# Gathering the first 42 chunks of edge rows from the raw input, and scaling them in their buffers

## The chip, the core and the metric

One core of one Trainium2 chip runs the whole program. The metric is the device time of one execution in microseconds (us); the median of three timed executions is quoted, and one further execution was taken with the hardware profiler. The engines have the profile's names: PE (matrix), PEld (its weight loads), DVE (vector), ACT (scalar), POOL (GpSimd) and SP (which here only issues DMAs).

## What is computed

`x` has 6250 rows (nodes) of 256 floats. `src` and `dst` list 106250 directed edges, sorted by `dst`. With `ln` a row normalization without gain:

```python
y    = ln(x)
h    = segment_sum((y @ W)[src] * rsqrt(max(out_deg, 1))[src], dst) * rsqrt(max(in_deg, 1)) + b
x2   = x + relu(h)
out  = x2 + moe(ln(x2))      # 8 experts, top 2 of them for each row, 256 -> 1024 -> 256 with gelu
```

`out_deg` counts how often a node stands in `src`, `in_deg` how often in `dst`. The matrix product with `W` is linear, so the kernel sums scaled rows of `y` first and multiplies by `W` after the sum.

## The kernel before

**Prologue (the source count).** All 831 chunks of 128 source numbers (the last holds 10) are loaded as `flat`. DVE splits each number into a low part (7 bits) and a high part (0 to 48), and for 32 chunks at a time (26 rounds, `counts`) writes two one-hots: `oh_hi` (L305, 128 x 1568, bf16) and `oh_lo` (L310, 128 x 4096, bf16), each in two buffers. PE multiplies the two, chunk by chunk, into `hist` (L316), a 128 x 49 table of out-degrees that lies in one PSUM tile. Beside this ACT takes the sums of the 49 tiles of `x` (`xres`, L368), then the sums of squares (L378); PE turns the edge lists by transposes (`turn`, L332, eight turns) so that `srcT` (row numbers, one column for each chunk) and `relT` (position of the target in a 128-wide window) come out with edges on partitions; POOL turns the integer lists into floats (`s_f` L274, `dst_f` L275) and makes small constants (`after`, `ones`, `tok1`, ...). In the fourth turn (`n == 3`) a product with `ones` gives `total` (L394), the number of edges that lie within their windows. The order on each engine is the order of the program text (`manual_schedule`).

When `hist` is complete, DVE works out a scale and a shift for each node (`scale0`, `shift0`, L418 and L420). DVE, ACT and POOL scale the 49 tiles of `xres` in place (L429, L434, L424), and SP writes them in seven groups to the DRAM table `ytab` (L436). Then all engines read `flag_i` and pass a branch (L443) that handles edges outside of their windows; with this input it isn't taken.

**Edge phase.** 831 chunks of 128 edges follow, 14 to a block, 60 blocks. For chunk i POOL gathers 128 rows of `ytab` by an indirect DMA into `msg[i % NMSG]` (`gather`, L1064); column 256 of every `msg` tile is 1. DVE makes one-hots of the window positions for seven chunks at a time (`oh`, L1075). PE adds `oh`.T @ `msg` into `pm` (L1135, 128 x 257: sums and in-degree). After each block `finish` (L600 to L612) transposes `pm` into a ring of node columns; when a tile of 128 nodes is complete, `tile_sums` (L646, L650) multiplies by `W`; when a group of tiles is complete, `route_group` chooses experts, and its rows are sent to the DRAM table `xs` by indirect DMAs on POOL (L825). The experts' products (`ph` L996, `py` L1013) are woven between the chunks at a planned rate, and their results are added to `out` by indirect DMAs on POOL (L1035).

POOL's order is written out by the main loop: `gather(0..11)` ahead of it, and then, at chunk i, `gather(i + LEAD)` with `LEAD = 12`, followed by at most one of the waiting `xs` sends or `out` adds. `NMSG` is 28. A gather waits until the matmul that read its buffer before is done.

**Tail.** When the edges are used up, the remaining expert steps run back to back.

Of the kernel before, what the change touches and what calls it, by code (L numbers as in the profile page):

```python
# [23 lines left out]
def gnn_then_moe(  # L24
# [47 lines left out]
    MW = D + 4  # L72
    NMSG = 28
    LEAD = 12
# [76 lines left out]
    split = LASTROWS // 32 * 32  # L151

    edges = ctx.enter_context(tc.tile_pool(name="edges", bufs=1))
    srcT = edges.tile([P, NCOL], I32, name="srcT")
# [31 lines left out]
    xres = early.tile([P, NT, D], F32, name="xres")  # L186
    dst_f = early.tile([NBE, BE], F32, name="dst_f")
    inside = early.tile([NBE, BE], F32, name="inside")
    flag_i = early.tile([1, 1], I32, name="flag_i")
    starts = list(range(0, NCP, GC))  # L190

    with tc.manual_schedule(), tc.tile_pool(
# [14 lines left out]
        iota_hi = hl.tile([P, NHI, GC], BF16, name="iota_hi")  # L207
        in_rows = {n: rows.tile([NBE, BE], I32, name=f"{n}_rows") for n in ("src", "dst")}
        zeros = const.tile([P, SB * XW], F32, name="zeros")
# [6 lines left out]
        nc.vector.memset(zeros, 0.0)  # L216

        nc.sync.dma_start(flat[:, :FULL], src[: FULL * P].rearrange("(p c) -> p c", p=P))
# [4 lines left out]
        for name, v in (("src", src), ("dst", dst)):  # L223
            nc.scalar.dma_start(
                in_rows[name][: NBE - 1, :],
                v[: (NBE - 1) * BE].rearrange("(p c) -> p c", c=BE),
            )
            nc.scalar.dma_start(
                in_rows[name][NBE - 1 : NBE, :LASTE],
                v[(NBE - 1) * BE :].rearrange("(p c) -> p c", p=1),  # L230
            )
# [40 lines left out]
        steps_of(pcol, [[0, 1]], 0, 1)  # L272
        s_f = rows.tile([NBE, BE], F32, name="s_f")
        nc.gpsimd.tensor_copy(s_f, in_rows["src"])  # L274
        nc.gpsimd.tensor_copy(dst_f, in_rows["dst"])  # L275
        steps_of(iota_w, [[1, WIN]])
        after = const.tile([P, P], F32, name="after")
        nc.gpsimd.memset(after, 1.0)
# [15 lines left out]

        for op, by, to in ((ALU.bitwise_and, LO - 1, lo), (ALU.logical_shift_right, 7, hi)):
            part = rows.tile([P, NCP], I32, tag="part", name="part")
            nc.vector.tensor_scalar(part, flat, by, None, op0=op)
            nc.vector.tensor_copy(to, part)
        hist = s1h.tile([P, NT], F32, name="hist")
# [36 lines left out]

        counts(14)

# [36 lines left out]
        for n, one in enumerate(turns):  # L375
            turn(*one)
            for _, t in zip(range(share), squares):
                nc.scalar.activation(junk, xres[:, t, :], AF.Square,  # L378
                                     bias=mean_n[:, t : t + 1], accum_out=sqs[:, t : t + 1])
            counts(1)  # L380
            if n == 3:

                wrow = rowsp.tile([1, P], F32, tag="wrow", bufs=1, name="wrow")
                nc.tensor.transpose(wrow[:, :NBE], win_f, ident[:NBE, :NBE])
                within = rows.tile([NBE, 1], F32, name="within")
                nc.vector.tensor_scalar(
                    inside, rel, 0.0, float(WIN - 1), op0=ALU.max, op1=ALU.min
                )
# [27 lines left out]
        nc.vector.tensor_scalar(deg, hist, 1.0, None, op0=ALU.max)  # L416
        scale0 = rsqrt(rows, deg, NT, "ns")
        nc.vector.tensor_tensor(scale0, scale0, rs0, ALU.mult)  # L418
        shift0 = rows.tile([P, NT], F32, name="shift0")
        nc.vector.tensor_tensor(shift0, mean_n, scale0, ALU.mult)  # L420
        for g in range(NG):
            for t in range(g * GT, (g + 1) * GT):
# [15 lines left out]
                xres[:, g * GT : (g + 1) * GT, :],  # L438
            )


# [96 lines left out]
    ringp = ctx.enter_context(tc.tile_pool(name="ring", bufs=2))  # L538
    msgp = ctx.enter_context(tc.tile_pool(name="msg", bufs=1))
    selp = ctx.enter_context(tc.tile_pool(name="sel", bufs=3))  # L540
# [26 lines left out]
    nc.vector.memset(gone_to[0], 0.0)  # L567
    msg = [msgp.tile([P, MW], F32, name=f"msg{i}") for i in range(NMSG)]
    for i in range(NMSG):
        nc.vector.memset(msg[i][:, D : D + 1], 1.0)  # L570
    scatters, bases, adds, reads = [], [], [], []
# [671 lines left out]
```

## Time and profile before

| | us |
|---|---|
| median of three executions | 1839.8 (1833.39 to 1840.7) |
| the profiled execution, device time | 1838.93 |
| its span in the profile | 1837.1 |
| last scale and shift ready, scaling of `xres` begins | 114.25 |
| first gather is issued on POOL | 138.13 |
| first `pm` matmul | 145.32 |
| first send to `xs` | 311.39 |
| last `pm` matmuls | 1535 |

How to read it: the span is what the profiler covers from the first instruction to the last, and it lies 1.8 us under the device time of the same execution. A row of the timeline begins with its start and its duration in us, and a bracket at its end tells how long the engine had been idle and what ended that. A row of the windows' table has each engine's busy time in the stretch with the number of instructions, then the granted PE clock as a share of full speed (PEclk), the DMA engines' busy share and the rate in GB/s. The list of waits has total us, number of waits and the longest. Busy PE time is modelled: a matmul at the lower clock shows as a longer one.

### The profile page before, as it was taken

How to read it: one execution, taken by the hardware profiler on the slowest of the kernel's cores; microseconds unless marked ns; L12 is line 12 of the kernel's file. 1: busy time of each engine (PE TensorE's matmuls, PEld its weight loads, DVE VectorE, ACT ScalarE, POOL GpSimd, SP SyncE). 2: the span in 40 equal slices, each digit the busy share in tenths (PEclk: the TensorE clock that was granted, in tenths of full speed). 3: DMA queues.
4: the chain of work that ended last, by engine and by line, in shares of the span. 5: the costliest groups of instructions: out<-in, count | busy, mean ns of one | idle time of the engine just before them, and what ended most of it. 6: DMA issues, size and time to landing. Idle time of an engine off the chain costs nothing.

```text
span 1837.1 us, 21552 instructions
## 1 busy us (share of the span) xinstructions
PE 1525.5 (83%) x7076; PEld 1245.8 (68%) x7076; DVE 822.4 (45%) x2971; ACT 340.8 (19%) x869; POOL 1112.2 (61%) x1063
## 2 busy tenths in 40 slices
PE   6846786666798688797987989999798977999996
PEld 6833344344587577676876878878687865788885
DVE  9961226145136237264363363735545476321111
ACT  2740001001112102121120121212112121222221
POOL 1007776776774776776767767777777773222222
PEclk9998777676798799898998999999999987999998
DMA  4645433343663664655756748576576642756662
GB/s 144 250 142 180 114 112 111 101 151 96 220 207 118 187 215 150 203 175 183 223 152 213 219 152 280 168 221 215 164 215 201 218 153 60 239 181 201 209 193 68
DMA packets 119173, 321.68 MB, mean 175 GB/s; under 512 B 20918, under 2 KB 74100, under 8 KB 112140
## 3 DMA queue, kind: packets, MB, share of 16 engines
q1 hardware_dynamic: 58784, 183.17, 27.9%
q0 software_dynamic: 60144, 136.19, 27.4%
q8 instruction: 59, 0.97, 0.2%
q10 hardware_dynamic: 124, 0.85, 0.1%
q14 instruction: 62, 0.51, 0.1%
HBM read 268.07 MB, written 52.05 MB: 174 GB/s over the span
## 4 chain that ended last, share of the span: by engine, by line
PE 57%; DMA 15%; DVE 11%; issue 5%; POOL 3%; ACT 1%; POOLq 0%; DVEq 0%; ACTq 0%
PE ph L996 18%; PE py L1013 17%; PE pm L1135 14%; DMA msg<-ytab,srcT 11%; POOL msg L1064 3%; DMA xs<-rowt,pos_i 2%; DMA out_x<-yo,to_i 2%; PE misc L646 2%; PE misc L714 1%; PE misc L723 1%; PE ptf L952 1%; PE misc L606 1%; DVE xeT L972 1%; PE misc L607 1%; PE misc L650 1%
## 5 line engine op out<-in xcount | busy, mean ns | idle before, releaser
L1064 POOL DMA_INDIRECT msg<-ytab,srcT x831 | 818.6, 985 | 272.6 <-issue 128.0
L1135 PE MATMUL pm<-msg,oh 128*128 128x257 f32 x1662 | 570.1, 439 | 148.1 <-DMA msg<-ytab,srcT 135.4
L1135 PEld LDWEIGHTS pm<-msg,oh 128*128 128x128 f32 x1662 | 330.4, 214 | 267.9 <-DMA msg<-ytab,srcT 168.1
L996 PE MATMUL ph<-xeT,w 128*128 128x256 f32 x1728 | 442.7, 395 | 59.1 <-DVE xeT L972 59.0
L1013 PE MATMUL py<-w,hT 128*128 128x256 f32 x1728 | 436.0, 388 | 0.0
L996 PEld LDWEIGHTS ph<-xeT,w 128*128 128x128 f32 x1728 | 339.4, 199 | 112.2 <-DVE xeT L972 64.7
L1013 PEld LDWEIGHTS py<-w,hT 128*128 128x128 f32 x1728 | 327.8, 195 | 41.6 <-DVE yb L1024 0.6
L1003 ACT ACTIVATE hT<-ph,w 128x256 f32<-128x256 f32 x432 | 180.7, 470 | 797.5 <-PE ph L996 627.6
L1035 POOL DMA_INDIRECT out_x<-yo,to_i x108 | 174.9, 1619 | 253.1 <-DVE yo L1029 227.5
L612 DVE TENSOR_TENSOR ring<-ring,misc 128x384 f32 x60 | 33.3, 555 | 411.9 <-PE misc L607 411.5
L825 POOL DMA_INDIRECT xs<-rowt,pos_i x98 | 101.7, 1038 | 87.7 <-issue 46.1
L1075 DVE TENSOR_TENSOR oh<-iota_w,relT 128x896 f32<-128x896 f32 (+1 forms) x119 | 126.6, 1077 | 33.4 <-PE pm L1135 32.8
L960 DVE SCALAR_TENSOR_TENSOR to_i<-xin,to 128x2 int32<-128x2 f32 x54 | 8.9, 164 | 258.1 <-DMA out_x<-yo,to_i 257.0
L316 PE MATMUL hist<-oh_hi,oh_lo 128*128 128x49 bf16 x831 | 85.0, 279 | 21.4 <-DVE oh_lo L310 21.2
L316 PEld LDWEIGHTS <-oh_lo 128*128 128x128 bf16 x831 | 81.5, 150 | 24.0 <-DVE oh_lo L310 23.2
L600 ACT COPY ag<-pm 128x257 f32<-128x257 f32 x60 | 22.5, 374 | 345.0 <-PE pm L1135 306.3
L1024 DVE TENSOR_TENSOR yb<-py,w 128x512 f32<-128x512 f32 x54 | 37.1, 688 | 68.0 <-PE py L1013 67.9
L646 PE MATMUL misc<-gw_sb,ring 128*128 128x256 f32 x196 | 56.4, 413 | 6.6 <-DVE ring L612 6.6
L310 DVE TENSOR_TENSOR oh_lo<-iota_lo,src_lo 128x4096 bf16<-128x4096 bf16 x26 | 59.4, 2286 | 0.0
L972 DVE TENSOR_SCALAR xeT<-ptf,w 128x256 f32<-128x256 f32 x108 | 53.7, 539 | 9.3 <-PE ptf L952 9.3
L725 ACT COPY xtT<-misc 128x256 f32<-128x256 f32 x49 | 18.2, 372 | 180.1 <-PE misc L723 180.1
L646 PEld LDWEIGHTS misc<-gw_sb,ring 128*128 128x128 f32 x196 | 38.7, 205 | 18.6 <-DVE ring L612 13.6
(531 smaller groups left out, 1054.5 us busy)
## 6 DMA issues: line engine op xcount, KB each, us to landing
w<-in_wcat SPq DMA_DIRECT2D x54, 2182.0 KB, 9.3
xin<-xs SPq DMA_DIRECT2D x54, 260.0 KB, 3.7
msg<-ytab,srcT POOLq DMA_INDIRECT x831, 2.9
strayT<-zeros SPq DMA_DIRECT2D x1, 9216.0 KB
ytab<-xres SPq DMA_DIRECT2D x7, 896.0 KB, 6.8
ring<-strayT SPq DMA_DIRECT2D x4, 1536.0 KB
x<-in_x SPq DMA_DIRECT2D x48, 128.0 KB, 10.2
out_x<-x SPq DMA_DIRECT2D x48, 128.0 KB, 2.1
```

Of the source, the lines that this page charges most:

```text
L310: nc.vector.tensor_tensor(oh_lo, iota_lo, lo[:, None, c0 : c0 + GC].to_broadcast([P, LO, GC]), ALU.is_equal,)
L316: nc.tensor.matmul(hist, oh_lo[:, :, c], oh_hi[:, :, c], start=(c0 + c == 0), stop=(c0 + c == NCH - 1),)
L646: nc.tensor.matmul(pw[:, :D], sums[:, k, c0 : c0 + P], gw_sb[:, k, :], start=(k == 0), stop=(k == KD - 1),)
L825: sc = nc.gpsimd.indirect_dma_start(out=xs, out_offset=bass.IndirectOffsetOnAxis(ap=pos_i[:, j : j + 1], axis=0), in_=rowt[:, i, :], in_of ...
L972: nc.vector.tensor_scalar(xeT[:, k, :], pt[:, k, :], w[:, OG + k : OG + k + 1], w[:, OB + k : OB + k + 1], op0=ALU.mult, op1=ALU.add,)
L996: nc.tensor.matmul(ph[:, c - c0, :], w[:, k * H + c * P : k * H + (c + 1) * P], xeT[:, k, :], start=(k == 0), stop=(k == KD - 1),)
L1003: nc.scalar.activation(hT[:, c, :], ph[:, c - c0, :], AF.Gelu, bias=w[:, OB1 + c : OB1 + c + 1],)
L1013: nc.tensor.matmul(py[:, s, :], hT[:, c, s * P : (s + 1) * P], w[:, OW2 + c * D : OW2 + (c + 1) * D], start=(c == 0), stop=(c == HC - 1),)
L1035: ad = nc.gpsimd.indirect_dma_start(out=out, out_offset=bass.IndirectOffsetOnAxis(ap=to_i[:, s : s + 1], axis=0), in_=yo[:, s, :], in_offs ...
L1064: nc.gpsimd.indirect_dma_start(out=msg[i % NMSG][:, :D], out_offset=None, in_=ytab, in_offset=bass.IndirectOffsetOnAxis(ap=srcT[:, c : c + ...
L1075: nc.vector.tensor_tensor(oh[:, :n, :], iota_w[:, None, :].to_broadcast([P, n, WIN]), relT[:, c : c + n, None].to_broadcast([P, n, WIN]), ...
L1135: nc.tensor.matmul(pm, oh_of[b, half][:, j % HALF, :], msg[i % NMSG][:, : D + 1], start=(j == 0), stop=(i + 1 == end_of[b]),)
```

## The change

The first 42 chunks are gathered from `x` itself, not from `ytab`, and POOL issues these gathers early in the prologue, as soon as their row numbers are there. The rows arrive unscaled, so each needs scale and shift of its source node. These are picked for each edge with one-hots: 42 transposed low-part one-hots (`loT`) select by a matmul the 2 x 49 candidates, and a product with the high-part one-hot (`ohe_hi`) and a sum leave one value. The float32 table is split into three bf16 parts that are added in PSUM.

- The row numbers come by their own small load, `first_i` (42 x 128), first on ACT's queue; ACT turns them into floats, PE transposes them, ACT writes them back as integers (`firstT`).
- `NMSG` becomes 42. The `msg` tiles are allocated at the start; POOL sets their column of ones behind the 42 gathers, where DVE did it after the branch.
- The casts of the edge lists go from POOL to ACT, in place. Their loads are split in 48 and 11 rows.
- Between the fifth and the sixth round of the count DVE makes the one-hots of the 42 chunks, PE transposes them, ACT copies them out of PSUM.
- The product with `ones` (`total`) moves from the fourth turn to the sixth.
- Behind the scaling of `xres`, nine groups of up to five chunks are picked and scaled, a third of the chunks on DVE, the others on ACT.
- In the main loop the first 42 gathers are gone; `gather(i + LEAD)` begins with `gather(42)` at i = 30.

```diff
-    NMSG = 28
+    NMSG = 42
...
+        first_i = rows.tile([NMSG, P], I32, name="first_i")
+        nc.scalar.dma_start(first_i, src[: NMSG * P].rearrange("(c p) -> c p", p=P))
...
-            nc.scalar.dma_start(
-                in_rows[name][: NBE - 1, :],
-                v[: (NBE - 1) * BE].rearrange("(p c) -> p c", c=BE),
-            )
+            for b0, b1 in ((0, 48), (48, NBE - 1)):
+                nc.scalar.dma_start(
+                    in_rows[name][b0:b1, :],
+                    v[b0 * BE : b1 * BE].rearrange("(p c) -> p c", c=BE),
+                )
...
-        nc.gpsimd.tensor_copy(s_f, in_rows["src"])
-        nc.gpsimd.tensor_copy(dst_f, in_rows["dst"])
         steps_of(iota_w, [[1, WIN]])
+        first_f = rows.tile([NMSG, P], F32, name="first_f")
+        nc.scalar.copy(first_f, first_i)
+        ptF = rowsp.tile([P, 4, P], F32, tag="ptE", name="ptF")
+        nc.tensor.transpose(ptF[:, 0, :NMSG], first_f, ident[:NMSG, :NMSG])
+        firstT = rows.tile([P, NMSG], I32, name="firstT")
+        nc.scalar.copy(firstT, ptF[:, 0, :NMSG])
+        nc.scalar.copy(s_f, in_rows["src"])
+        nc.scalar.copy(dst_f, in_rows["dst"])
+        for i in range(NMSG):
+            nc.gpsimd.indirect_dma_start(
+                out=msg[i][:, :D], out_offset=None, in_=x,
+                in_offset=bass.IndirectOffsetOnAxis(ap=firstT[:, i : i + 1], axis=0),
+            )
+        for i in range(NMSG):
+            nc.gpsimd.memset(msg[i][:, D : D + 1], 1.0)
...
-        counts(14)
+        counts(5)
+        ident_b = rows.tile([P, P], BF16, name="ident_b")
+        nc.vector.tensor_copy(ident_b, ident)
...
+        digits(firstT, lo_e, hi_e, NMSG)
...
+        for c0 in range(0, NMSG, GC):
+            n = min(GC, NMSG - c0)
+            oh_lo = s1o.tile([P, LO, GC], BF16, tag="oh_lo", name="oh_lo")
+            nc.vector.tensor_tensor(
+                oh_lo[:, :, :n], iota_lo[:, :, :n],
+                lo_e[:, None, c0 : c0 + n].to_broadcast([P, LO, n]), ALU.is_equal,
+            )
+            nc.vector.tensor_tensor(
+                ohe_hi[:, :, c0 : c0 + n], iota_hi[:, :, :n],
+                hi_e[:, None, c0 : c0 + n].to_broadcast([P, NHI, n]), ALU.is_equal,
+            )
+            for d0 in range(0, n, 4):
+                m = min(4, n - d0)
+                ptb = rowsp.tile([P, 4, P], BF16, tag="ptB", name="ptB")
+                for d in range(d0, d0 + m):
+                    nc.tensor.transpose(ptb[:, d - d0, :], oh_lo[:, :, d], ident_b)
+                nc.scalar.copy(loT[:, c0 + d0 : c0 + d0 + m, :], ptb[:, :m, :])
+        counts(9)
...
-            if n == 3:
+            if n == 5:
...
+        for q in range(3):
+            nc.vector.tensor_copy(parts[q], rest if q else both)
+            if q < 2:
+                nc.vector.tensor_tensor(rest, rest if q else both, parts[q], ALU.subtract)
...
+        PK = 5
+        per_edge = rows.tile([P, NMSG, 2], F32, name="per_edge")
+        for c0 in range(0, NMSG, PK):
...
+            for c in range(n):
+                for q in range(3):
+                    nc.tensor.matmul(
+                        pk[:, c], loT[:, c0 + c, :], parts[q], start=(q == 0), stop=(q == 2)
+                    )
+            prod = rows.tile([P, PK, 2, NT], F32, tag="prod", name="prod", bufs=2)
+            nc.vector.tensor_tensor(
+                prod[:, :n], pk,
+                ohe_hi[:, :, c0 : c0 + n].rearrange("p t c -> p c t")[:, :, None, :]
+                .to_broadcast([P, n, 2, NT]), ALU.mult,
+            )
+            nc.vector.tensor_reduce(per_edge[:, c0 : c0 + n, :], prod[:, :n], AX.X, ALU.add)
+            for c in range(c0, c0 + n):
+                if c % 3 == 0:
+                    nc.vector.tensor_scalar(
+                        msg[c][:, :D], msg[c][:, :D], per_edge[:, c, 0:1],
+                        per_edge[:, c, 1:2], op0=ALU.mult, op1=ALU.add,
+                    )
+                else:
+                    nc.scalar.activation(msg[c][:, :D], msg[c][:, :D], AF.Identity,
+                                         bias=per_edge[:, c, 1:2], scale=per_edge[:, c, 0:1])
...
-    for i in range(LEAD):
-        gather(i)
...
         if i + LEAD < NCK:
-            gather(i + LEAD)
+            if i + LEAD >= NMSG:
+                gather(i + LEAD)
```

More of the change, by code (lines that the diff above doesn't have):

```diff
@@ L151, in gnn_then_moe @@
     split = LASTROWS // 32 * 32
+    msgp = ctx.enter_context(tc.tile_pool(name="msg", bufs=1))
+    msg = [msgp.tile([P, MW], F32, name=f"msg{i}") for i in range(NMSG)]
+    assert NMSG <= NCH - 1 and NMSG <= 2 * GC
     edges = ctx.enter_context(tc.tile_pool(name="edges", bufs=1))
@@ L186, in gnn_then_moe @@
     xres = early.tile([P, NT, D], F32, name="xres")
-    dst_f = early.tile([NBE, BE], F32, name="dst_f")
-    inside = early.tile([NBE, BE], F32, name="inside")
+    in_rows = {n: early.tile([NBE, BE], I32, name=f"{n}_rows") for n in ("src", "dst")}
+    s_f, dst_f = (in_rows[n][:].bitcast(F32) for n in ("src", "dst"))
+    inside = s_f
     flag_i = early.tile([1, 1], I32, name="flag_i")
@@ L207, in gnn_then_moe @@
         iota_hi = hl.tile([P, NHI, GC], BF16, name="iota_hi")
-        in_rows = {n: rows.tile([NBE, BE], I32, name=f"{n}_rows") for n in ("src", "dst")}
         zeros = const.tile([P, SB * XW], F32, name="zeros")
@@ L272, in gnn_then_moe @@
         steps_of(pcol, [[0, 1]], 0, 1)
-        s_f = rows.tile([NBE, BE], F32, name="s_f")
-        nc.gpsimd.tensor_copy(s_f, in_rows["src"])
-        nc.gpsimd.tensor_copy(dst_f, in_rows["dst"])
         steps_of(iota_w, [[1, WIN]])
+        first_f = rows.tile([NMSG, P], F32, name="first_f")
[13 more added lines that the diff above has]
+            nc.gpsimd.memset(msg[i][:, D : D + 1], 1.0)
         after = const.tile([P, P], F32, name="after")
@@ L292, in gnn_then_moe, with digits @@
         steps_of(step_no, [[1, MMAX]])
[L295 to L298, printed above, removed]
+        def digits(v, lo, hi, n):
+            for op, by, to in ((ALU.bitwise_and, LO - 1, lo), (ALU.logical_shift_right, 7, hi)):
+                part = rows.tile([P, NCP], I32, tag="part", name="part")[:, :n]
+                nc.vector.tensor_scalar(part, v, by, None, op0=op)
+                nc.vector.tensor_copy(to, part)
+        digits(flat, lo, hi, NCP)
         hist = s1h.tile([P, NT], F32, name="hist")
@@ L335, in turn @@
             nc.scalar.copy(to[:, j0 : j0 + m, :], pt[:, :m, :NBE])
-        counts(14)
+        counts(5)
+        ident_b = rows.tile([P, P], BF16, name="ident_b")
+        nc.vector.tensor_copy(ident_b, ident)
+        lo_e = rows.tile([P, NMSG], BF16, name="lo_e")
+        hi_e = rows.tile([P, NMSG], BF16, name="hi_e")
+        digits(firstT, lo_e, hi_e, NMSG)
+        loT = rows.tile([P, NMSG, P], BF16, name="loT")
+        ohe_hi = rows.tile([P, NHI, NMSG], BF16, name="ohe_hi")
+        for c0 in range(0, NMSG, GC):
[16 more added lines that the diff above has]
+        counts(9)
         late = rows.tile([NBE, 1], F32, name="late")
@@ L416, in gnn_then_moe @@
         nc.vector.tensor_scalar(deg, hist, 1.0, None, op0=ALU.max)
-        scale0 = rsqrt(rows, deg, NT, "ns")
-        nc.vector.tensor_tensor(scale0, scale0, rs0, ALU.mult)
-        shift0 = rows.tile([P, NT], F32, name="shift0")
+        both = rows.tile([P, 2, NT], F32, name="both")
+        scale0, shift0 = both[:, 0, :], both[:, 1, :]
+        nc.vector.tensor_tensor(scale0, rsqrt(rows, deg, NT, "ns"), rs0, ALU.mult)
         nc.vector.tensor_tensor(shift0, mean_n, scale0, ALU.mult)
+        rest = rows.tile([P, 2, NT], F32, name="rest")
+        parts = [rows.tile([P, 2, NT], BF16, name=f"part{q}") for q in range(3)]
+        for q in range(3):
+            nc.vector.tensor_copy(parts[q], rest if q else both)
+            if q < 2:
+                nc.vector.tensor_tensor(rest, rest if q else both, parts[q], ALU.subtract)
         for g in range(NG):
@@ L439, in gnn_then_moe @@
             )
+        PK = 5
+        per_edge = rows.tile([P, NMSG, 2], F32, name="per_edge")
+        for c0 in range(0, NMSG, PK):
+            n = min(PK, NMSG - c0)
+            pk = rowsp.tile([P, 4, P], F32, tag="ptE", name="pk").rearrange("p a b -> p (a b)")[
+                :, : n * 2 * NT
+            ].rearrange("p (c h t) -> p c h t", c=n, h=2)
+            for c in range(n):
[19 more added lines that the diff above has]
+                                         bias=per_edge[:, c, 1:2], scale=per_edge[:, c, 0:1])
     n_stray = nc.values_load(flag_i[0:1, 0:1], min_val=0, max_val=NCOL * P)
@@ L538, in gnn_then_moe @@
     ringp = ctx.enter_context(tc.tile_pool(name="ring", bufs=2))
-    msgp = ctx.enter_context(tc.tile_pool(name="msg", bufs=1))
     selp = ctx.enter_context(tc.tile_pool(name="sel", bufs=3))
@@ L567, in gnn_then_moe @@
     nc.vector.memset(gone_to[0], 0.0)
-    msg = [msgp.tile([P, MW], F32, name=f"msg{i}") for i in range(NMSG)]
-    for i in range(NMSG):
-        nc.vector.memset(msg[i][:, D : D + 1], 1.0)
     scatters, bases, adds, reads = [], [], [], []
```

## Prediction

> **What bounds the kernel now.** I began with the windows, cut at the stages: prologue, table and branch, edges before and after the first routing, edges with experts, tail.
>
> ```profile
> 0.00:115.00 115.00, 89.39 (x862) 85.47 (x862) 105.92 (x121) 58.95 (x207) 13.26 (x20) 1.00 0.46 158
> 115.00:145.00 30.00, 0.00 (x0) 0.00 (x0) 13.84 (x57) 6.24 (x13) 9.29 (x12) 1.00 0.85 287
> 145.00:311.00 166.00, 127.38 (x354) 73.73 (x354) 55.40 (x194) 8.16 (x22) 123.29 (x125) 0.75 0.41 123
> 480.00:1540.00 1060.00, 931.11 (x4292) 786.09 (x4292) 513.81 (x2083) 194.94 (x455) 777.86 (x740) 0.93 0.61 190
> 1540.00:1837.00 297.00, 271.96 (x1270) 237.95 (x1270) 75.97 (x309) 63.87 (x152) 62.97 (x42) 0.95 0.55 171
> ```
>
> The prologue is DVE's (106 of 115 us), with POOL idle for 100 us of it. From 145 to 311 nothing looks full. POOL's timeline shows why:
>
> ```profile
> 138.13 1.18 POOL L1064 DMA_INDIRECT msg<-ytab,srcT  x1 [19.49 <-SPq L443]
> 145.32 2.05 PE L1135 MATMUL pm<-msg,oh 128*128 128x257 f32 x4 [34.51 <-DMA msg<-ytab,srcT]
> 192.98 0.95 POOL L1064 DMA_INDIRECT msg<-ytab,srcT  x1 [0.31 <-issue]
> 194.24 0.95 POOL L1064 DMA_INDIRECT msg<-ytab,srcT  x1 [0.30 <-issue]
> 311.39 1.01 POOL L825 DMA_INDIRECT xs<-rowt,pos_i  x1 [5.30 <-issue]
> ```
>
> A gather takes 0.95 us and the next begins 0.30 us later: POOL is full at 1.26 us a chunk though its busy share reads 0.76. PE waits for it:
>
> ```profile
> PE pm L1135 <- DMA msg<-ytab,srcT: 61.7, 45, 34.5
> ```
>
> (waits of PE from 145 to 312; 34.5 us of them is the wait for the first chunk.) PE could go faster: six chunks that lay ready at 151.94 took 3.83 us, 0.64 each at full clock; at 210.71, in a stretch with gaps, three took 3.16, 1.05 each. So POOL sets the pace until the first routing. There it stops: at 311.39 it waits 5.3 us for positions that PE, DVE and ACT work out behind chunk 97.
>
> **What it removes.** From POOL's edge queue, 42 gathers. The 42 gathers before 194.24 are the ones taken out (the windows count 42 from 137 to 194), so gather 42 begins at 194.24 now. In the changed program it is the first on POOL behind the branch, and waits only for its buffer: for the first `pm` matmul, which ends 0.9 us after it begins. If that matmul came at 145.3 as now, gather 42 would come at 146.2, 48.0 us sooner. From there POOL's order is what it was, LEAD still 12, so whatever gather 42 gains is kept as long as POOL paces: **gain = 48.0 - d**, d being what the prologue adds ahead of the first `pm`.
>
> Does PE keep up? It must be through chunk 97 when gather 97 lands, 55 x 1.26 + 4 = 73 us after the first `pm`. A block is 14 x 0.64 + 1.3 (two transposed groups, 0.63 and 0.64) + about 1.3 for tiles (L646 1.13, L650 0.38 each) = 11.5 us, 0.82 a chunk, 80 us for 98, if all of these rows, taken from half-clock stretches, stay; at 0.75 it is even with POOL. So PE may cost up to 7 us; at 1.05 a chunk throughout it would cost 30. I take 0.
>
> Later stages keep the shift: order of chunks, sends, adds and experts is unchanged, and the ring of 28 or 42 never binds with a lead of 12. The tail's work is the same.
>
> **What it adds to the prologue (d).**
>
> ```profile
> 16.80 2.28 DVE L310 TENSOR_TENSOR oh_lo<-iota_lo,src_lo 128x4096 bf16<-128x4096 bf16 x1
> 28.56 1.82 POOL L274 CAST s_f<-src_rows 60x1792 f32<-60x1792 int32 x1 [20.57 <-DMA src_rows<-in_src]
> 29.15 2.07 DVE L305 TENSOR_TENSOR oh_hi<-iota_hi,src_hi 128x1568 bf16<-128x1568 bf16 x1 [0.34 <-PE hist L316]
> 114.25 10.67 DVE L429 TENSOR_SCALAR xres<-xres,ns_r,shift 128x256 f32<-128x256 f32 x28
> ```
>
> 1. *PE's head.* The transpose of `first_f` now stands first on PE, and all of `hist` behind it. ACT makes `first_f` only after issuing its loads, the last of which wait for the first two `x` loads: the trace has these landing at 8.97 and, but for one part, 11.55. With ACT's table load (1.28 us) and two small copies PE starts at 15.0 instead of 12.55: +2.4. Bound: ACT was held in its last issue until 23.8; were it again, +14.
> 2. *The edge one-hots.* DVE: one `oh_lo` and `oh_hi` in full (3.3) and one of 10/32 (1.0), casts 0.9. PE's transposes go through two PSUM buffers that ACT empties eleven times; the relT copy of 240 numbers takes 0.60, so 0.7 each for 512; the sixth count round waits for the first eight. Walked through with two buffers, that round ends at 38.9 instead of 31.3 (28.0 for the fifth, and one round of 3.3): +7.6. Two rounds get 1.1 us back each, as POOL's casts no longer hold DVE (the row at 29.15 took 2.07 where others take 0.97): +5.4 in all (4 to 8). Here ACT must have its casts done, and for that `dst` must have landed. Before, 59 rows landed at 28.5 (`src`) and 49.2 (`dst`), 413 KB in 20.6 us; 896 KB of `x` on 128 rows landed within 7.3. I take the 48 rows to be nearer to the latter; if not, ACT, the copies, PE and `hist` stand until 53: about +21.
> 3. *POOL is late for `total`.* `ones` is set behind the 42 gathers and 42 memsets (42 x 0.06 by DVE's row for them, 2.5), PE waits for it in the sixth turn, with `hist` rounds behind. When does POOL get there? Gathers beside DVE:
>
> ```profile
> 187.27 2.06 DVE L1075 TENSOR_TENSOR oh<-iota_w,relT 128x896 f32<-128x896 f32 x2
> 188.37 1.79 POOL L1064 DMA_INDIRECT msg<-ytab,srcT  x1 [0.30 <-PE pm L1135]
> 190.47 0.95 POOL L1064 DMA_INDIRECT msg<-ytab,srcT  x1 [0.30 <-DMA msg<-ytab,srcT]
> ```
>
> A gather that begins under a DVE product of two SBUF tensors stands until that ends and then takes 0.83; it gets in even between two that stand back to back (139.62: 1.22). In the count DVE does nothing else, `oh_hi` 0.9 then `oh_lo` 2.2 us. A gather let in when `oh_lo` ends is done 0.83 later, and the next asks after 1.13: too late for the end of `oh_hi`, unless DVE paused 0.33 for PE, as in every second round. So three gathers in two rounds (6.6 us): 23 by the end of the fourteenth round (65), 5 more by the turns (77), two a turn (4 us each): 40 by 101, done at 104, `ones` at 109, where PE wanted it at 104: +5. With one a round it is +17; with 1.26 us throughout, done at 68, 0.
>
> The Trainium skill speaks against this placing: "SBUF — State Buffer", "Who interferes with whom", says that a GpSimd instruction reading SBUF fully blocks beside such a DVE operation, and the page's summary advises against hiding a POOL-issued DMA under DVE's fast modes. By its example (3.1 us for a DMA beside a DVE copy, 0.62 alone), an estimate of 3.4 us a gather leaves 16 for after 103 and makes this term 20, the sum 1818. The trace's gathers wait only for the instruction under way; that decides.
>
> 4. *Three bf16 parts*: five operations of about 0.24: +1.2.
> 5. *Picking and scaling*, behind the scaling of `xres`: 8.4 groups on DVE, each a product of 490 (nearest row: 512 in 0.69), a sum of 490 (nearest: 40 in 0.18; by length 0.7), 1.67 scalings at 0.38 to 0.41: 2.07 us, 17.4 in all; then `oh` 1.05 and a start, 18.9 from the last scaling to the first `pm`. Now it is 145.32 - 124.92 = 20.4 (table landing, branch, gather): -1.5. The table's writes hide most of it: they held the branch until 137.4. Without reductions at that speed +5; at least 12.5 (branch) + 1.8, so -6. ACT's 28 scalings at 0.50 (14) run beside. PE's 126 small products fit between.
>
> Sum: d = 2.4 + 5.4 + 5 + 1.2 - 1.5 = 12.5. Gain 48.0 - 12.5 = 35.5; the profiled execution was 1838.9 (span 1837.1 and 1.8 around it), 0.9 under the median. So 1803.
>
> **Rivals.**
> - *A smaller gain*: one gather a round (+12), or PE at 0.95 a chunk (93 us against 73 to chunk 97, -20): gain 24 to 16, 1815 to 1823. For it: PE's clock share of 0.75 here. Against: the gaps that go with it are POOL's.
> - *The loads don't split*: terms 1 and 2 become 14 and 21 with overlap, d about 34, 1825.
> - *Slower*: gathers get in only when DVE pauses. About 12 would be through at the sixth turn, and PE stands for 30 x 1.26 + 5 = 43 us: d = 50; with the chain of term 5 at +5 it is 57, so 1848. It decides from d = 48. For it: the gather stretched to 1.79. Against: the back-to-back rows.
> - *No effect on the end*: the head start is given back at 311, where POOL waits for routing. Against: that wait ends a chain from chunk 97, which itself waited for its gather (266.8, landing 269.5).
>
> **How the numbers follow.** Forecast (gain 25 to 47) 0.63; smaller gain or unsplit loads 0.20; slower 0.09; given back within 9 us 0.08, a part of which may fall on either side. About 0.5% (9 us) is what a measurement of this kernel can tell from no change. All low bounds together (0 from term 1, 4, 0, 1.2, -6) give d = -1, 1790; the high end takes in one gather a round with a PE cost, and unsplit loads: 1826.
>
> **What would show it.** In the profile after: `hist` beginning near 15; `dst` landed before 20; 42 gathers from 15 on, three in two rounds, ended near 104; `total` waiting for POOL about 5 us; scaling of `xres` at 126; first `pm` near 157, gather 42 within 1 us of it and then 1.26 us apart; first send near 275; last `pm` near 1500; a tail as long as now. It is wrong if gathers in the count take over 3.3 us each, if PE and not POOL paces chunks 42 to 97, or if the distance from the first send to the end is not 1526 us.

## The result and the profile after

| | before | after |
|---|---|---|
| median, us (13 runs each, side by side) | 1840.70 | 1821.32 |
| lowest to highest, us | 1833.39 to 1850.43 | 1811.36 to 1830.20 |
| the profiled execution, us | 1838.93 | 1816.55 |
| its span, us | 1837.1 | 1814.8 |
| mean granted PE clock | 0.903 | 0.918 |

The ratio is 0.9894, with a 95% interval of 0.9872 to 0.9915: the changed kernel is about 1.1% (19 us; 22 in the profiled pair) faster. The prediction was 1803, a gain of 36; its range, 1790 to 1826, holds the result. So the direction was right and the size was not.

The windows of the changed kernel, cut at the same stages (the prologue to the scaling, the picks, the edges to the first send, the edges with experts, the tail; columns as before):

```profile
0.00:138.00 138.00, 96.36 (x906) 90.73 (x907) 109.06 (x129) 68.21 (x222) 94.42 (x102) 1.00 0.54 171
138.00:172.00 34.00, 11.79 (x127) 10.50 (x126) 32.73 (x65) 21.22 (x42) 3.79 (x7) 1.00 0.60 194
172.00:290.00 118.00, 96.60 (x355) 67.35 (x356) 57.98 (x197) 8.16 (x22) 86.44 (x88) 0.84 0.46 143
459.00:1518.00 1059.00, 927.32 (x4282) 782.29 (x4280) 514.03 (x2077) 194.80 (x455) 776.39 (x740) 0.94 0.61 191
1518.00:1815.00 297.00, 272.01 (x1270) 237.70 (x1270) 75.92 (x309) 63.88 (x152) 62.92 (x42) 0.95 0.55 171
```

The stage from the first chunk to the first send took 166 us and takes 118. The last two windows, set 21 and 22 us earlier than those of the kernel before, have the same busy times as there (POOL 776 and 778, PE 927 and 931; in the tail PE 272 and 272). The prologue and the picks take 172 where the prologue and the wait for the table took 145. POOL, idle for 100 us of the old prologue, is now busy for 94 us of it. In the timelines of PE and POOL of the changed kernel (start, duration, instruction) these are the first `pm` matmuls, gathers 42 and 90, and the first send:

```profile
171.86 9.50 PE L1216 MATMUL pm<-msg,oh 128*128 128x257 f32 x32 [6.11 <-DVE oh L1157]
173.33 1.18 POOL L1146 DMA_INDIRECT msg<-ytab,srcT  x1 [31.55 <-PE pm L1216]
235.97 0.95 POOL L1146 DMA_INDIRECT msg<-ytab,srcT  x1 [0.30 <-issue]
289.64 1.04 POOL L907 DMA_INDIRECT xs<-rowt,pos_i  x1 [4.02 <-issue]
```

The first `pm` is at 171.86 (before 145.32). Gather 42, now POOL's first, follows at 173.33, where it stood at 194.24: 20.9 us earlier. PE runs through 16 chunks that lie ready in the first row, and the 42 chunks take it 23.3 us, 0.556 each. By chunk 90 it has caught up with POOL: gather 90 begins at 235.97, its matmul at 238.8. The first send is 21.8 us earlier (311.39 to 289.64), the last `pm` 22.1 (1535.0 to 1512.9), the end 22.3. PE's waits between the first chunk and the first send:

```profile
PE pm L1216 <- DMA msg<-ytab,srcT: 9.2, 17, 1.1
```

This wait for gathered rows was 61.7 us with the first chunk. It is 9.2, and POOL still sets the pace behind it.

Where the missing 14 us are is seen in the prologue. PE's waits up to the first `pm`:

```profile
PE ptF L286 <- ACT first_f L284: 19.6, 1, 19.6
PE total L444 <- POOL ones L305: 11.1, 1, 11.1
```

PE's first instruction waits until 19.6 for ACT, and `total` waits 11.1 us for `ones`. ACT's timeline shows the first of the two (ACTq is the issue of a DMA):

```profile
17.63 0.23 ACTq L236 DMA_DIRECT2D dst_rows<-in_dst  x1
17.89 1.28 ACT L284 ACT_TABLE_LOAD   x1 [17.89 <-DMA xres<-in_x]
19.19 0.30 ACT L284 CAST first_f<-first_i 42x128 f32<-42x128 int32 x1
22.92 1.73 ACT L290 CAST dst_rows<-dst_rows 60x1792 f32<-60x1792 int32 x1 [1.14 <-DMA dst_rows<-in_dst]
```

The last load of `dst` rows waited for the second group of `x` until 17.63, and `first_f` stands behind it. `dst` had landed by 22.92, where it landed at 49.2 in the kernel before: the split loads came in time.

### The profile page after: what moved, and what is told of

Its sections match the earlier page's. It is cut to its first block, busy times and chain, and to the rows that moved or that the text cites. A ratio compares the mean times of both kernels' runs of the same rounds, so it can differ in the third digit from the quotient of the medians.

```text
span 1814.8 us, 22012 instructions
## 1 busy us (share of the span) xinstructions
PE 1512.6 (83%) x7245; PEld 1252.7 (69%) x7245; DVE 847.4 (47%) x2989; ACT 365.0 (20%) x912; POOL 1149.8 (63%) x1103
## 4 chain that ended last, share of the span: by engine, by line
PE 58%; DMA 13%; DVE 11%; issue 5%; POOL 2%; ACT 1%; DVEq 0%; POOLq 0%; ACTq 0%
PE ph L1078 19%; PE py L1095 17%; PE pm L1216 15%; DMA msg<-ytab,srcT 10%; PE misc L728 2%; DMA out_x<-yo,to_i 1%; DMA xs<-rowt,pos_i 1%; POOL msg L1146 1%; PE misc L796 1%; PE misc L805 1%; PE ptf L1034 1%; PE misc L688 1%; PE misc L689 1%; DVE xeT L1054 1%; POOL xs L907 1%
## 5 line engine op out<-in xcount | busy, mean ns | idle before, releaser
L1146 POOL DMA_INDIRECT msg<-ytab,srcT x789 | 777.5, 985 | 272.3 <-issue 121.6
L1216 PE MATMUL pm<-msg,oh 128*128 128x257 f32 x1662 | 542.4, 426 | 102.9 <-DMA msg<-ytab,srcT 85.2
L1095 PE MATMUL py<-w,hT 128*128 128x256 f32 x1728 | 431.3, 385 | 0.0
L1095 PEld LDWEIGHTS py<-w,hT 128*128 128x128 f32 x1728 | 323.7, 192 | 41.6 <-DVE yb L1106 0.5
L1157 DVE TENSOR_TENSOR oh<-iota_w,relT 128x896 f32<-128x896 f32 (+1 forms) x119 | 126.7, 1077 | 21.5 <-PE pm L1216 21.1
L292 POOL DMA_INDIRECT msg<-in_x,firstT x42 | 84.4, 2010 | 24.8 <-issue 12.5
L1054 DVE TENSOR_SCALAR xeT<-ptf,w 128x256 f32<-128x256 f32 x108 | 53.7, 539 | 8.9 <-PE ptf L1034 8.9
```

Source lines behind the costliest of these rows:

```text
L292: nc.gpsimd.indirect_dma_start(out=msg[i][:, :D], out_offset=None, in_=x, in_offset=bass.IndirectOffsetOnAxis(ap=firstT[:, i : i + 1], axi ...
L1054: nc.vector.tensor_scalar(xeT[:, k, :], pt[:, k, :], w[:, OG + k : OG + k + 1], w[:, OB + k : OB + k + 1], op0=ALU.mult, op1=ALU.add,)
L1095: nc.tensor.matmul(py[:, s, :], hT[:, c, s * P : (s + 1) * P], w[:, OW2 + c * D : OW2 + (c + 1) * D], start=(c == 0), stop=(c == HC - 1),)
L1146: nc.gpsimd.indirect_dma_start(out=msg[i % NMSG][:, :D], out_offset=None, in_=ytab, in_offset=bass.IndirectOffsetOnAxis(ap=srcT[:, c : c + ...
L1157: nc.vector.tensor_tensor(oh[:, :n, :], iota_w[:, None, :].to_broadcast([P, n, WIN]), relT[:, c : c + n, None].to_broadcast([P, n, WIN]), ...
L1216: nc.tensor.matmul(pm, oh_of[b, half][:, j % HALF, :], msg[i % NMSG][:, : D + 1], start=(j == 0), stop=(i + 1 == end_of[b]),)
```

## Experiments

All are edits of the changed kernel. The theory is that of the prediction, gain = 48.0 - d, with d made too small in its terms 1, 3 and 5. The rival is that the shorter prologue doesn't reach the end, or that the terms overlap and don't add up.

The first four runs (`e1_head` to `e4_no_stt`) were made on a chip on which the kernel before took 2246 us, with PE's clock granted at 0.84; their times can't be set beside the others, but their prologues can, since DVE's, ACT's and POOL's rows there have the same durations (`oh_lo` 2.28, a gather alone 0.95).

### ACT's copies ahead of the waiting loads (e1_head)

`row_loads` and `last_row` hold the row loads as they were; the last two of `dst` (11 rows and 522 numbers) now stand behind the two copies:

```diff
+        row_loads("src", src, slice(0, 2))
+        last_row("src", src)
+        row_loads("dst", dst, slice(0, 1))
...
         nc.scalar.copy(firstT, ptF[:, 0, :NMSG])
+        row_loads("dst", dst, slice(1, 2))
+        last_row("dst", dst)
         nc.scalar.copy(s_f, in_rows["src"])
```

> Made from the changed kernel: ACT copies first_f and firstT before it issues the last two loads of dst rows (11 rows and 522 ids), so the transpose at the head of PE's queue no longer waits for loads of x. Theory (step 1 of the sum is mis-sized because ACT's two issues stand behind x groups 0 and 1): first_f is done by about 7, hist starts near 12.6 as in the kernel before, instead of 19.86, and the gathers start near 9 instead of 20.45. The prologue gains the 7.3 us of hist, and 4 to 6 us more because the gathers end some 12 us earlier and total waits for ones 5 to 7 us instead of 11.1: first pm at 158 to 161 instead of 171.9, median near 1809. Rival A (PE's first step is not what the prologue hangs on, the DVE's one-hots are): first pm stays above 168, median near 1820. Rival B (the prologue gets shorter but the end does not follow it): first pm falls as in the theory, the median stays near 1821.

Measured: 2233.5 us, ratio to the kernel before on that chip 0.9987 (0.9935 to 1.0039). PE's timeline at the start:

```profile
7.52 0.33 PE L292 MATMUL ptF<-ident,first_f 42*128 42x42 f32 x1 [7.52 <-POOL ident masks.py:199]
12.54 3.68 PE L348 MATMUL hist<-oh_hi,oh_lo 128*128 128x49 bf16 x35 [4.69 <-DVE oh_lo L342]
```

`hist` begins at 12.54, as in the kernel before, and the first `pm` comes at 161.9 instead of 171.9. Of these 9.9 us, 7.3 are the head, and nearly all of the rest is a shorter wait of `total` (8.6 instead of 11.1; 5 to 7 were expected, so the first `pm` lies just outside 158 to 161). Term 1 is confirmed; rival A falls. On that chip the end didn't follow, which is what rival B said. PE's waits from 160 to 330, and the rows of ACT and PE at the longest of them ("issue" and "remote" stand where the profile shows nothing that ended the wait):

```profile
PE misc L696 <- issue: 46.6, 3, 21.1
```

```profile
198.66 0.38 ACT L690 COPY ag<-pm 128x257 f32<-128x257 f32 x1 [27.46 <-remote]
199.09 0.69 PE L696 MATMUL misc<-ident,ag 128*128 128x128 f32 x2 [21.05 <-issue]
```

PE stood three times, up to 21.1 us. Each time it went on 0.06 us after ACT's copy of a finished block's sums (`ag`), which PE transposes. In the rows shown the copy began 20.6 us after PE's matmuls had ended (178.03), with ACT idle; what held it the profile doesn't show. Between the stops PE wasn't always slower: 28 `pm` matmuls in a row took 6.23 us here as in the profile after. From 200 to 250 its clock was granted at 0.74, where the profile after has 0.81, and chunk 120 was multiplied 48.6 us after its gather began (274.1 to 322.7), in the profile after 10.7 (273.8 to 284.5). From the first `pm` to the first send 165.9 us passed, 48 more than the 117.8 of the profile after, and the three stops make up 46.6. So the edges hung on PE there and not on POOL, as in the prediction's rival of a slow PE, but by these stops, which that rival didn't have; that the lower clock causes them isn't shown. The changed kernel itself wasn't run on that chip. Nor do the four runs made there order by their first `pm`: it is at 161.9, 162.3, 174.0 and 177.6 for ratios of 0.9987, 0.990, 0.9934 and 0.9938.

### `ones` ahead of the gathers (e2_ones)

```diff
         steps_of(iota_w, [[1, WIN]])
+        ones = const.tile([P, P], F32, name="ones")
+        nc.gpsimd.memset(ones, 1.0)
```

> Made from the changed kernel: POOL fills ones before the 42 early gathers and not after them. Nothing else moves. Theory (step 3: total waits for ones, which stand behind the gathers on POOL): the wait of total for ones, 11.1 us, is gone, flag_f no longer waits 7.1 us, hist ends 9 to 11 us earlier, first pm at 161 to 163, median near 1811. The early gathers then have no pause of DVE to end in and end after 117. Rival (something else is just as late there, the gathers' landing, ACT's squares or the count's own pace): first pm stays above 168, median near 1821.

Measured: 2224.7 us, ratio 0.990 (0.9855 to 0.9945), first `pm` at 162.3, 9.5 us earlier. `total` is gone from the list of PE's waits. The early gathers end at 120.9, later than the 117.35 of the changed kernel, and without effect. The theory holds for the prologue, and term 3 is a wait on POOL's order, not on the gathered rows.

### `ohe_hi` laid out for its reader (e3_flat)

```diff
-        ohe_hi = rows.tile([P, NHI, NMSG], BF16, name="ohe_hi")
+        ohe_hi = rows.tile([P, NMSG, NHI], BF16, name="ohe_hi")
...
-                ohe_hi[:, :, c0 : c0 + n], iota_hi[:, :, :n],
+                ohe_hi[:, c0 : c0 + n, :].rearrange("p c t -> p t c"), iota_hi[:, :, :n],
```

> Made from the changed kernel: ohe_hi is stored as chunks x digits, so that prod reads its second operand with consecutive elements instead of 42 elements apart. Theory (step 5: prod took 1.21 us for 490 elements, not 0.69, because of that stride): prod takes 0.65 to 0.75 us, the nine products together 4 us less; the two one-hots that write ohe_hi may take up to 1.5 us more; first pm near 169, median near 1818.5. Rival (the 1.21 us belongs to a product of an f32 operand with a bf16 one, or to reading pk): prod stays at 1.2 us, first pm at 172 to 174.

Measured: 2237.6 us, ratio 0.9934 (0.9886 to 0.9981), first `pm` at 174.0, later and not earlier. DVE's timelines, of the changed kernel's first pick and then of this kernel's first one-hot and first pick:

```profile
148.95 1.20 DVE L511 TENSOR_TENSOR prod<-pk,ohe_hi 128x490 f32<-128x490 f32 x1
150.19 0.66 DVE L516 TENSOR_REDUCE per_edge<-prod 128x10 f32<-128x490 f32 x1
```

```profile
35.62 7.55 DVE L377 TENSOR_TENSOR ohe_hi<-iota_hi,hi_e 128x1568 bf16<-128x1568 bf16 x1
155.43 0.66 DVE L511 TENSOR_TENSOR prod<-pk,ohe_hi 128x490 f32<-128x490 f32 x1
```

The theory was right on the reader: 490 products take 0.66 us with consecutive operands and 1.20 with the one-hot read 42 elements apart. It was wrong on the writer: 1568 one-hots written 49 elements apart took 7.55 us, where they took 0.97, and the second one-hot took 2.43 instead of 0.41. What the picks gained was lost at the start.

### The other instruction under the long gathers (e4_no_stt)

Two of the 42 early gathers of the changed kernel took 8.06 and 8.63 us, the others 0.94 to 2.95. Both began under a `scalar_tensor_tensor` of 60 x 1792 elements.

```profile
74.25 8.06 POOL L292 DMA_INDIRECT msg<-in_x,firstT  x1 [0.30 <-issue]
104.96 8.63 POOL L292 DMA_INDIRECT msg<-in_x,firstT  x1 [0.30 <-issue]
```

The edit puts other instructions in place of the two:

```diff
-        nc.vector.scalar_tensor_tensor(
-            rel, rel, w_f, dst_f, op0=ALU.subtract, op1=ALU.add
-        )
+        nc.vector.tensor_scalar(rel, rel, w_f, None, op0=ALU.subtract)
+        nc.vector.tensor_tensor(rel, rel, dst_f, ALU.add)
...
+                nc.vector.tensor_tensor(inside, inside, rel, ALU.is_equal)
+                nc.vector.tensor_reduce(within, inside, AX.X, ALU.add)
```

> Made from the changed kernel: the two scalar_tensor_tensor instructions on 60 x 1792 elements (rel, inside) are replaced by a tensor_scalar and a tensor_tensor (rel), and by a tensor_tensor and a tensor_reduce (inside), of the same shapes. Theory (the early gathers that began under them took 8.06 and 8.63 us because of that kind of instruction): no early gather takes over 3.5 us, the 42 end near 106 instead of 117.3, total waits for ones 0 to 2 us instead of 11.1, and against that DVE works 2 to 3 us longer: first pm at 163 to 166, median near 1814. Rival (any long two-operand f32 instruction does it, or the place in the schedule): gathers of 8 us are still there, first pm at 172 to 175, median 1821 to 1824.

Measured: 2239.5 us, ratio 0.9938 (0.9888 to 0.9987), first `pm` at 177.6. DVE and POOL side by side:

```profile
74.50 2.02 DVE L413 TENSOR_TENSOR rel<-rel,dst_rows 60x1792 f32<-60x1792 f32 x1
74.90 8.69 POOL L292 DMA_INDIRECT msg<-in_x,firstT  x1 [0.30 <-issue]
107.89 2.01 DVE L439 TENSOR_REDUCE within<-src_rows 60x1 f32<-60x1792 f32 x1
108.98 7.91 POOL L292 DMA_INDIRECT msg<-in_x,firstT  x1 [0.30 <-issue]
```

The gathers of 8.69 and 7.91 us are there, one begun under a product and one under a reduction. The kind of instruction isn't the cause, and since a reduction has only one large operand, of the rival's two readings the place in the schedule is the one left. Its first `pm` of 172 to 175 was missed: `total` waited 15.6 us for `ones` here.

### The three edits together (best42)

These are the edits of `e1_head` and `e2_ones` with a third. Here `ohe_hi` is written with consecutive elements as well as read so, from an iota (a row of counting numbers) of the 49 digits that is broadcast over the chunks:

```diff
+        iota_t = rows.tile([P, NHI], BF16, name="iota_t")
+        steps_of(iota_t, [[1, NHI]])
...
+                ohe_hi[:, c0 : c0 + n, :], iota_t[:, None, :].to_broadcast([P, n, NHI]),
+                hi_e[:, c0 : c0 + n, None].to_broadcast([P, n, NHI]), ALU.is_equal,
```

> Made from the changed kernel, three edits together: first_f and firstT ahead of ACT's last two loads of dst rows, ones filled ahead of the early gathers, and ohe_hi written and read with consecutive elements, by an iota of 49 digits broadcast over the chunks. Theory (the prologue's three mis-sized terms add up): hist starts at 12.6 (7.3 us earlier than in the changed kernel), total has no wait (10 to 11 us), prod at 0.66 instead of 1.21 (4.6 us less, the one-hots some 1 us more): first pm at 149 to 153 instead of 171.9, the early gathers' stalls of 8 us still there and without effect, d = 4 to 8. Where POOL sets the pace from chunk 90 on, the end follows: ratio to the kernel before 0.977 to 0.980. Rival A (the terms share their time and do not add): first pm at 155 to 162, ratio 0.983 or more. Rival B (PE sets the pace of the main loop, as where its clock is granted at 0.84 in the runs so far): first pm as in the theory, ratio 0.985 to 0.995, no better than the run with ones alone.

Measured: 1798.4 us median against 1836.9, ratio 0.9784 (0.9746 to 0.9823): twice the gain of the changed kernel. Lines of its DVE, PE and POOL timelines:

```profile
28.91 1.78 DVE L387 TENSOR_TENSOR ohe_hi<-iota_t,hi_e 128x1568 bf16<-128x1568 bf16 x1
130.80 0.65 DVE L521 TENSOR_TENSOR prod<-pk,ohe_hi 128x490 f32<-128x490 f32 x1
149.32 8.83 PE L1226 MATMUL pm<-msg,oh 128*128 128x257 f32 x32 [5.54 <-DVE oh L1167]
150.80 1.18 POOL L1156 DMA_INDIRECT msg<-ytab,srcT  x1 [27.16 <-PE pm L1226]
```

The first `pm` is at 149.3, gather 42 at 150.80. Beside the kernel before on the same chip (first `pm` 145.6, gather 42 at 193.4, last `pm` 1534.9, span 1836.6), gather 42 is 42.6 us earlier, the last `pm` 45.3 (1489.6) and the end of the span 46.4 (1790.2). d is 3.7. The theory holds: the terms add, and the end follows.

### 28 early gathers (n28)

```diff
-    NMSG = 42
+    NMSG = 28
```

> The changed kernel with 28 message buffers and 28 early gathers instead of 42. Theory (gain = time of the first late gather before less that of first pm after): gather 28 stood at about 176 in the kernel before, so 30 us are to be had and not 48; d falls too: the 28 gathers end by about 80 to 85, total no longer waits for ones (10 to 11 us), and three groups of picks fewer (7.5 us), so first pm is at 151 to 155 and gather 28 within 2 us of it: as good as 42, ratio 0.987 to 0.991. Rival (the gain goes with the number of early gathers): two thirds of it, ratio 0.993, first pm above 160.

Measured: 1814.7 us, ratio 0.9867 (0.9829 to 0.9906), first `pm` at 150.1:

```profile
151.60 1.18 POOL L1146 DMA_INDIRECT msg<-ytab,srcT  x1 [24.83 <-PE pm L1216]
```

That is gather 28; in the kernel before it stood at 175.32, so 23.7 us are gained, slightly more than with 42. Fewer gathers leave less to gain and shorten the prologue by as much: here `total` has no wait, since the 28 gathers end at 84.8.

### The changed kernel and the kernel before on that chip (after_again, before_again)

> The changed kernel unchanged, on the chip of this call, as the measure for the other two: first pm at 172, ratio to the kernel before 0.989 where POOL sets the pace. Where PE sets it (granted clock near 0.84), the theory expects less, 0.992 to 1.0, with the first gather into a used buffer just as early.

> The kernel before, for its trace on the chip of this call: first pm at 145. Where the chunks between 0 and 120 take the same 1.26 us each as in the profile of before, POOL sets the pace here too; where PE has long idle times with nothing that it waits for, as in the first runs, PE is the bound and hides what the early gathers bring.

Measured: 1819.1 us, ratio 0.9879 (0.9832 to 0.9926), first `pm` at 171.4, gather 42 at 172.9; the kernel before has its first `pm` at 145.6 and POOL's 1.26 us a chunk. Both repeat the first pair.

### Small instructions behind the long ones (e5_small)

```diff
+        def small_steps():
+            one = [rows.tile([NBE, 1], F32, tag=f"one{k}", name=f"one{k}") for k in range(5)]
+            nc.vector.tensor_copy(one[0], pcol[:NBE])
+            for k in range(4):
+                nc.vector.tensor_scalar(one[k + 1], one[k], 1.0, None, op0=ALU.add)
...
+        small_steps()
...
+                small_steps()
```

> Made from the changed kernel: behind each of the two scalar_tensor_tensor instructions on 60 x 1792 elements DVE runs five small instructions that depend on one another (60 x 1, about 1 us together); they compute nothing that is used. Theory (a gather that begins under a two-operand f32 instruction or a reduction isn't let in between one-hots that follow without a gap, but ends 0.7 to 0.8 us after the next gap or row of small instructions, as in all ten stalls of the runs so far): no gather takes over 4 us, the 42 end at 106 to 109 instead of 117.3, total waits for ones 0 to 3 us instead of 11.1; against that 2 us more of DVE: first pm at 162 to 166 instead of 171.9. Rival (only a pause in which DVE waits for another engine lets it in): gathers of 7 us and more are still there, first pm at 172 to 175.

Measured: 1816.7 us, ratio 0.9898 (0.9851 to 0.9945), first `pm` at 171.1. POOL's timeline and the small instructions on DVE's:

```profile
75.65 0.68 DVE L422 TENSOR_SCALAR one<-one 60x1 f32<-60x1 f32 x4
74.49 1.82 POOL L292 DMA_INDIRECT msg<-in_x,firstT  x1 [0.31 <-issue]
76.62 6.81 POOL L292 DMA_INDIRECT msg<-in_x,firstT  x1 [0.30 <-issue]
```

The gather under the long instruction is now let in by the small ones (1.82 us), but the next, begun under the one-hot behind them, took 6.81 and ended 0.8 us after the next small instruction (82.43 to 82.60). At the second place it was 2.44 and 6.67. The stall moved and didn't go away: `total` still waited 9.4 us for `ones`, and the first `pm` missed the theory's 162 to 166. So neither theory nor rival holds as written. The stalled gather stood through the two rounds of one-hots that DVE runs there without a wait, 76.3 to 82.4. That isn't the whole of it either, since in the first two rounds of the count, also without a wait, gathers did get in (in the run with three edits one that began at 10.53 took 2.80). What holds the gather stays open.

### Two edits, and the third alone (head_ones, flat2; before_last)

> Two of the three edits of best42: first_f and firstT ahead of ACT's last loads of dst rows, and ones ahead of the early gathers. Theory: 7.3 us of the head and 10 to 11 us of total, first pm at 153 to 155, 4 us later than best42 (149.3); ratio to the kernel before 0.979 to 0.982 where POOL sets the pace. Rival (the two waits overlap, as the single edits of 10.0 and 9.6 us leave open): first pm at 158 to 162.

> The third edit of best42 alone: ohe_hi written and read with consecutive elements by an iota of 49 digits that is broadcast over the chunks. Theory: prod at 0.66 us instead of 1.21, 4.6 us less over nine groups, the two one-hots 1.1 us more (2.44 instead of 1.38), which the wait of total for ones takes up or not: first pm at 167 to 169, ratio 0.985 to 0.988 where POOL sets the pace. Rival (the picks aren't on the path): first pm at 172.

> The kernel before, for its trace on the chip of this call. With a clock near 0.91: first pm at 145.5, gather 42 at 193 to 194, last pm at 1535, as in its earlier profiles. With a clock near 0.84, as in the first call: first pm at 145.5 as well, but long idle times of PE in the first 120 chunks, so that chunk 42 isn't multiplied earlier than in the changed kernel by the 20 us that POOL gains.

Measured: head and `ones` together 1799.7 us, ratio 0.9794 (0.975 to 0.9837), first `pm` at 153.9: 7.3 and 10.7 us add up, 4.6 us behind the run with three edits. The third edit alone gives 1811.2 us, ratio 0.9865 (0.9826 to 0.9905), but its first `pm` comes only at 170.2, outside the expected 167 to 169. PE's waits and POOL's timeline say why:

```profile
PE total L446 <- POOL ones L307: 14.9, 1, 14.9
```

```profile
57.11 2.93 POOL L294 DMA_INDIRECT msg<-in_x,firstT  x1 [0.30 <-issue]
60.34 3.06 POOL L294 DMA_INDIRECT msg<-in_x,firstT  x1 [0.30 <-issue]
63.71 2.98 POOL L294 DMA_INDIRECT msg<-in_x,firstT  x1 [0.30 <-issue]
```

In this run the gathers from 53.7 to 70.0 were let in once a round, 3.0 us each, where the changed kernel's alternate 0.95, 1.89 and 2.88. Each began just behind the start of an `oh_lo` and ended 0.83 us after its end. The 42 ended at 120.1 instead of 117.35, and `total` waited 14.9 us instead of 11.1: most of the 4.4 us that the picks gained (18.4 us from the last scaling to the first `pm` instead of 22.8) was taken there. Of the 1.7 us by which the first `pm` is earlier, 0.8 are an earlier start of `hist` (19.06 instead of 19.86), which this edit doesn't touch, and the ratio's interval is 0.8% wide: what the third edit brings alone is not shown. The kernel before in this group has its first `pm` at 145.8, gather 42 at 194.6, last `pm` at 1540.8.

## Why the prediction was right in kind and wrong in size

*Gain = 48.0 - d* held. In the profiled pair d was 26.5, and 48.0 - 26.5 = 21.5 against 20.9 at gather 42, 21.8 at the first send and 22.3 at the end. The missing 0.6 us is that gather 42 began 1.47 us after the first `pm`, not 0.9. The formula held at the other values of d too. Below, each run is set against the kernel before on the same chip: the head start is gather 42 there (gather 28 for the run with 28) less 0.9 us after its first `pm`, and the last column is the difference of the medians.

| run | first `pm` | head start less d | first late gather, earlier by | last `pm`, earlier by | median, less by |
|---|---|---|---|---|---|
| changed kernel | 171.9 | 21.5 | 20.9 | 22.1 | 19.4 |
| the same, second profile | 171.4 | 21.1 | 20.5 | 16.9 | 17.8 |
| 28 gathers | 150.1 | 24.3 | 23.7 | 25.5 | 22.2 |
| three edits | 149.3 | 43.1 | 42.6 | 45.3 | 38.5 |
| head and `ones` | 153.9 | 39.8 | 39.2 | 46.0 | 35.6 |
| third edit alone | 170.2 | 23.6 | 23.0 | 35.4 | 24.1 |
| small instructions | 171.1 | 22.7 | 22.1 | 31.2 | 18.7 |

The first late gather follows the formula to 0.6 us. The last `pm` scatters by 5 to 6 us from one execution to the next (1535.0, 1534.9 and 1540.8 in three profiles of the kernel before; the last three rows are set against the 1540.8). The medians lie 2 to 5 us below the formula in six of the seven rows, each within its own interval, so that a little of the head start may be lost on the way to the end.

Other parts of the prediction held in the profiled pair as well: PE's cost up to chunk 97 was nothing, the distance from the first send to the end was 1525.2 us (1526 forecast), and nothing was given back at the routing. What failed is the sizing of d, in its terms 1, 3 and 5. The range still held the result, in part by luck: neither of the causes that set its upper end came true, one gather a round with a PE cost and unsplit loads. The terms:

| term | forecast | measured | how it is read |
|---|---|---|---|
| 1 PE's head | 2.4 | 7.3 | `hist` at 19.86 instead of 12.55; back at 12.54 in e1_head |
| 2 edge one-hots | 5.4 | 5.2 | end of the fourteenth round 57.52 to 70.07, less term 1 |
| 3 `total` waits for POOL | 5 | 10.7 | `hist` complete 110.85 to 134.08, less terms 1 and 2; 9.5 in e2_ones |
| 4 three parts | 1.2 | 1.4 | 137.47 to 138.86 |
| 5 picks | -1.5 | 2.4 | last scaling to first `pm` 22.8 us instead of 20.4 |
| sum | 12.5 | 27.0 | 26.5 with 0.5 that the scaling of `xres` got shorter |

The rows behind the first and the last term, `hist` before and after, and the scaling of `xres` after (its row before is in the prediction):

```profile
12.55 13.05 PE L316 MATMUL hist<-oh_hi,oh_lo 128*128 128x49 bf16 x128 [12.55 <-DVE oh_lo L310]
```

```profile
19.86 16.68 PE L340 MATMUL hist<-oh_hi,oh_lo 128*128 128x49 bf16 x160
138.86 10.17 DVE L487 TENSOR_SCALAR xres<-xres,both 128x256 f32<-128x256 f32 x28
```

*Term 1* took the landing of the first two groups of `x` from the profile of before, 8.97 and 11.55. In the changed kernel ACT's loads that wait for them went out at 14.27 and 17.63. The only edits to the queues at that point are `first_i` and the split row loads, issued from 0.8 to 5.2; that these take the groups' share of the DMA engines is argued and wasn't tried by itself. The bound of +14 covered it, the value didn't.

*Term 2* was right to 0.2 us.

*Term 3* had the mechanism right: gathers wait for the DVE instruction under way, about three got in per two rounds, and `ones` came late for `total`. They took 2.01 us in the mean. The start was 5.4 us later than assumed, but PE also wanted `ones` later, at 108.3 instead of 104, so that nearly cancels. What the prediction didn't have are the two stalls of 8 us: the other 40 gathers took 1.69 us in the mean, and an estimate from that (the two at 1.69 as well, 13 us less) has the gathers end near 104 and `ones` come about when PE wanted it. So the forecast 5 us was too small by the stalls, and would have been too large without them. The rule of the Trainium skill weighed there ("SBUF — State Buffer", "Who interferes with whom") led the prediction, by an estimate of 3.4 us from one gather to the next, to a term of 20; the measured 2.31 us from one to the next (42 in 96.9 us) and 10.7 us lie between that and the forecast.

*Term 5* took the product from the row of a product with consecutive operands (0.69). The actual one read `ohe_hi` 42 elements apart and took 1.21 in each of the eight groups of five (0.57 in the last, of two chunks); with consecutive elements it takes 0.66, and then 18.5 us lie between the last scaling and the first `pm` in the run with three edits, where the prediction had 18.9. So only the price of this one product was wrong. The Trainium skill had a rule that the prediction didn't weigh: "SBUF — State Buffer", "Door 1: The DMA port swizzle", notes that consecutive accesses to one 16-byte line run at full rate and that each access to a new line pays, so that bf16 can be stepped through for free by up to 8 elements. The runs agree on the reader (a stride of 42 elements, 1.8 times as long), and for the writer they show far more than that: 7.55 us with a stride of 49 against 0.97 with the same operands and consecutive results.

Of the rivals, the smaller gain came in size but not in cause: PE took 0.556 us a chunk, not 0.95, in the profiled pair. On the chip with a granted clock of 0.84 the edges did hang on PE, but with stops at its hand-over to ACT that the profile doesn't explain. The loads did split. Slower, by gathers that get in only when DVE pauses, fits two gathers of 42.

## What to carry to other kernels

When DMA issues move into a stage that another engine fills, list what stands behind them on their queue and who waits for it: one constant, filled behind 42 gathers, cost half as much as all the early gathers brought in the end. Price an elementwise instruction by a row with the same strides, not only the same count. And when the sum has the form of a fixed head start less what is added ahead of it, look for the added terms first: three small edits to them doubled the gain.

## What the hardware did that was not expected

- A bf16 operand read with a stride (42 elements) made a product of 490 elements take 1.21 us instead of 0.66; a bf16 result written with a stride (49 elements) made 1568 comparisons take 7.55 us instead of 0.97. Broadcast along the last axis, with consecutive results, the same 1568 took 1.78.
- An indirect DMA issued beside DVE's count took 0.95 us or was held until the end of the DVE instruction under way, and twice in every trace with 42 early gathers it was held over a whole stretch of one-hots, 6.7 to 8.7 us. Taking away the instruction under which it began, or putting small ones behind it, moved the stall but didn't end it.
- On one chip, at a granted clock of 0.84 in the mean, PE waited 93.1 us in ten waits for ACT's copies of block sums, up to 49.6 us at a time, in the profile of `e1_head` (9.2 us in three waits, up to 4.4, in the profile after), and the copies themselves stood 200.0 us in 12 waits that ended with nothing that the profile shows. There early gathers with a first `pm` at 161.9 brought no gain over the kernel before that could be measured (0.9987, 0.9935 to 1.0039), while two runs with a later first `pm` came out 0.6 to 0.7% below it.
